# Numbering the nodes 8p+k: contiguous pieces in DRAM, strided turns on chip

## The chip, the cores and the metric

The kernel runs on one core of one Trainium2 chip. The metric is device time in microseconds (us) of one execution, the median over several runs; lower is better. Five engines work side by side, each on its own list of instructions: TensorE (PE; its loads of the stationary operand are listed apart as PEld), VectorE (DVE), ScalarE (ACT), GpSimd (POOL) and SyncE (SP). SP, ACT and POOL issue the transfers, which run on 16 DMA engines.

## The reference

Sixteen graphs of N = 1024 nodes with C = 128 features; x is [16, 1024, 128] and adj [16, 1024, 1024] with entries 0 or 1.

```
# layer 0: gated graph network, 4 steps
h = relu(layernorm(x))
for i in range(4):
    m = adj^T @ (h @ weight[i])
    h = GRU(m, h)                       # w_ih, w_hh, b_ih, b_hh of step i
x = x + h * nodemask
# layer 1: graph convolution, 4 steps
h = relu(layernorm(x))
for i in range(4):
    h = relu(adj @ (h @ W[i]) + b[i])
    h = batchnorm over all graphs and nodes, gamma[i], beta[i]
x = x + h                               # the result
```

## The kernel before

All is done by `exact_path` (L342); `general_path` stands behind a test at the end and isn't executed with these inputs. `P = C = 128` is the number of partitions, `NB = N // P = 8` blocks of nodes, `NH = 2` halves of 512 columns (`HALF`), `BH = 4` blocks in each.

A graph's features live in two forms. *By node*: a tile of 128 partitions x 1024, partition p holding 8 nodes of 128 features, block k in columns 128k to 128k+127. *By feature* (`hT`): partition c, a column for each node, 1024 columns. Before the change, block k of the form by node holds node 128k + p in partition p, so block k of `hT` is the columns 128k to 128k+127. A load of x (`load_x`, L531), a store of the middle x (`xmid_d`, L637), its reads at the end (`fetch_x`, L955) and the stores of the result (L1004) therefore move eight (four, for halves) pieces of 512 bytes for each partition.

**Recurrent part** (45 to 1237 us of the profiled execution). Two streams, `sa` and `sb`, each work on every second graph, and `half_step` lets one aggregate while the other computes its gates. In a half-step TensorE does, for one stream, eight turns of h (`features_times` with `w` None, L491: `nc.tensor.transpose` of a block of `hT` into PSUM), the aggregation (`aggregate`, L516: stationary operand from the turned h split in two f32r parts, streaming operand the rows of adj), and, for the other, the gates (L720), 24 matmuls of two instructions each. At step 0 the turns aren't needed, since h begins in the form by node. ACT and DVE compute the gates from PSUM (L730 to L738). POOL and SP keep the order in which the code is written; the other engines are ordered by the scheduler as it builds the program.

Around that, per graph: the rows of adj are first copied in DRAM (`copy_rows`, L556, by POOL) and loaded from there (`load_rows`, L562, by SP); the first two graphs load them directly (`load_rows_first`, L549). At step 1 `transpose_rows` casts each of the eight row tiles to bf16 on POOL (L575, two buffers `half1`), SP turns it with a transposing DMA (L576) into `adjT`, and POOL stores `adjT` (L775). The next graph's x is loaded by POOL (L531), normalised (`norm`, L586 to L597), and turned into the form by feature (`turn`, L611, copied from PSUM by ACT, L612). When a graph is done, `tail_norm` turns its h back (L621), multiplies by the mask and adds x (L624), stores the middle x (L637), normalises it and stores that as `ymid_d` (L641), in rows of 4 KB. VectorE also looks whether adj's values are exact (`look`, L570).

**Convolution part** (1237 to 1846 us). Four layers over all 16 graphs: SP loads the stored adjT (L873), DVE and ACT widen it (L878, L876), TensorE multiplies by the weights (L493) and aggregates (L516, L503); a barrier for the batch norm follows each layer. In the last layer `fetch_x` reads the middle x back.

**Tail** (1846 us to the end). The last h is scaled (L897), turned (L1001), added to the middle x (L1003), and SP stores it in 32 transfers of 256 KB (L1004).

The tag `x` of the pool `keep` has four buffers (`flat`): x of the first graphs, the weights `w_g` at the start, later x of the following graphs.

Of the kernel before, what the change touches and what calls it, by code (L numbers as in the profile page):

```python
# [8 lines left out]
F32 = mybir.dt.float32  # L9
# [7 lines left out]
P = 128  # L17
HALF = 512
# [323 lines left out]
def exact_path(  # L342
# [21 lines left out]
    nc = tc.nc  # L364
    B, N, C = x.shape
    L = g_weight.shape[0]
    NB = N // P
    NH = N // HALF
    BH = HALF // P
# [4 lines left out]
    dram = ctx.enter_context(tc.tile_pool(name="dram", bufs=1, space=bass.MemoryType.DRAM))  # L374
# [7 lines left out]
    def tmp(name):  # L382
        return ps_t.tile([P, HALF], F32, tag="tmp", name=name)

    adjT_d = [dram.tile([P, NB, N], BF16, tag=f"adjT{b}", name=f"adjT_d{b}") for b in range(B)]
    xmid_d = [dram.tile([N, C], F32, tag=f"xmid{b}", name=f"xmid_d{b}") for b in range(B)]
    ymid_d = [dram.tile([P, N], F32, tag=f"ymid{b}", name=f"ymid_d{b}") for b in range(B)]

    def flat(name):
        return keep.tile([P, NB, C], F32, tag="x", name=name, bufs=4)  # L390
# [4 lines left out]
    def half_tile(name):  # L395
        return keep.tile([P, N], BF16, tag="half", name=name, bufs=8)

    def turned_tile(name):
        return keep.tile([P, NB, N], BF16, tag="adjT", name=name, bufs=1)
# [5 lines left out]
    ident = const.tile([P, P], F32, tag="ident", name="ident")  # L405
# [10 lines left out]
    maskT = const.tile([P, B * NB], F32, tag="maskT", name="maskT")  # L416
# [14 lines left out]
    def load_small(prep):  # L431

        vn = prep.tile([P, C], F32, tag="vn", name="vn", bufs=1)[:NV, :]
        r0 = 0
        for src in (g_b_ih, g_b_hh):
            nc.scalar.dma_start(vn[r0 : r0 + 3 * L, :], src.rearrange("l (g c) -> (l g) c", c=C))
            r0 += 3 * L
        for src in (c_b, c_gamma, c_beta):
            nc.scalar.dma_start(vn[r0 : r0 + L, :], src)
            r0 += L  # L440
        mn = prep.tile([P, P], F32, tag="mn", name="mn", bufs=1)
        nc.scalar.dma_start(mn, nodemask.rearrange("b (k p) -> (b k) p", p=P))
        return vn, mn

    def turn_small(vn, mn):
        pt = tmp("pt_v")
        nc.tensor.transpose(pt[:, :NV], vn, ident[:NV, :NV])
        nc.vector.tensor_copy(vecs, pt[:, :NV])
        nc.vector.tensor_add(brz, vecs[:, : 3 * L], vecs[:, 3 * L : 6 * L])
        pt = tmp("pt_m")  # L450
        nc.tensor.transpose(pt[:, :P], mn, ident)
        nc.vector.tensor_copy(maskT, pt[:, : B * NB])

    wns = {}
# [29 lines left out]
    def features_times(w, hT, hw, g, name):  # L484

        pt = tmp(f"hw_{name}_{g}")
        for q in range(BH):
            j = g * BH + q
            src = hT[:, j * P : (j + 1) * P]
            if w is None:  # L490
                nc.tensor.transpose(pt[:, q * P : (q + 1) * P], src, ident)  # L491
            else:
                nc.tensor.matmul(pt[:, q * P : (q + 1) * P], src, w, start=True, stop=True)  # L493
        cols = slice(g * HALF, (g + 1) * HALF)
        nc.scalar.copy(hw[0][:, cols], pt)  # L495
        nc.vector.tensor_sub(hw[1][:, cols], pt, hw[0][:, cols].bitcast(F32))  # L496
# [28 lines left out]
    with ExitStack() as st:  # L525
# [2 lines left out]

        def load_x(b, eng):
            xt = flat(f"x{b}")  # L530
            eng.dma_start(xt, x[b].rearrange("(k p) c -> p k c", p=P))  # L531
            return xt

        raws = {}

        def gru_row(b, j):
            if j < 6:
                return row_tile(f"row{b}_{j}")
            return work.tile([P, N], F32R, tag="row2", name=f"row{b}_{j}", bufs=4)

        def load_rows_first(b, stage):

            fs = []
            for j in range(NB):
                if j < 4:
                    f = stage[:, 2 * j : 2 * j + 2, :].rearrange("p a n -> p (a n)")
                else:
                    f = work.tile([P, N], F32, tag="h", name=f"first{b}_{j}", bufs=7)
                nc.sync.dma_start(f, adj[b][j * P : (j + 1) * P, :])  # L549
                fs.append(f)  # L550
            return fs

# [5 lines left out]
        def load_rows(b):  # L558
            ts = []
            for j in range(NB):  # L560
                t = gru_row(b, j)
                nc.sync.dma_start(t.bitcast(F32), raws[b][j * P : (j + 1) * P, :])  # L562
                ts.append(t)
            return ts

# [6 lines left out]
        def transpose_rows(b, row, j, adjT):  # L572

            t = work.tile([P, N], BF16, tag="half1", name=f"half{b}_{j}", bufs=2)
            nc.gpsimd.tensor_copy(t, row.bitcast(F32))  # L575
            nc.sync.dma_start_transpose(adjT[:, :, j * P : (j + 1) * P], t)  # L576

        def norm(xt, y, name):
# [3 lines left out]
        def norm_stats(xt, name):  # L582
            stats = small.tile([P, NB, 6], F32, tag="ln_st", name=f"st_{name}")
            mv = small.tile([P, NB, 2], F32, tag="ln_mv", name=f"mv_{name}")
            for k in range(NB):
                nc.vector.bn_stats(stats[:, k, :], xt[:, k, :])  # L586
                nc.vector.bn_aggr(mv[:, k, :], stats[:, k, :])
            return mv
# [14 lines left out]
        def turn(y, name, hT=None):  # L603

            if hT is None:
                hT = work.tile([P, N], F32, tag="h", name=f"h_{name}", bufs=7)
            for hf in range(NH):
                pt = tmp(f"pt_{name}_{hf}")
                for q in range(BH):
                    k = hf * BH + q  # L610
                    nc.tensor.transpose(pt[:, q * P : (q + 1) * P], y[:, k * P : (k + 1) * P], ident)  # L611
                nc.scalar.copy(hT[:, hf * HALF : (hf + 1) * HALF], pt)  # L612
            return hT

        def tail_norm(b, xt, hT):

            for hf in range(NH):
                pt = tmp(f"pt_x{b}_{hf}")
                for q in range(BH):
                    k = hf * BH + q  # L620
                    nc.tensor.transpose(pt[:, q * P : (q + 1) * P], hT[:, k * P : (k + 1) * P], ident)  # L621
                for q in range(BH):
                    k = hf * BH + q
                    nc.vector.scalar_tensor_tensor(  # L624
                        xt[:, k, :],
                        pt[:, q * P : (q + 1) * P],
                        maskT[:, b * NB + k : b * NB + k + 1],
                        xt[:, k, :],
                        ALU.mult,
                        ALU.add,  # L630
                    )
            mv = norm_stats(xt, f"mid{b}")
            if b + 1 < B:
                y = work.tile([P, N], F32, tag="h", name=f"y_mid{b}", bufs=7)
            else:
                y = xt.rearrange("p k c -> p (k c)")
            nc.gpsimd.dma_start(xmid_d[b].rearrange("(k p) c -> p k c", p=P), xt)  # L637

            def rest():
                norm_apply(xt, y, f"mid{b}", mv)  # L640
                nc.gpsimd.dma_start(ymid_d[b], y)  # L641

            return rest
# [157 lines left out]
        with tc.tile_pool(name="prep", bufs=1) as prep, tc.manual_schedule(engines=every):  # L801


            pt = tmp("pt_idle")
# [54 lines left out]
    pt = tmp("pt_flag")  # L859
# [74 lines left out]
    xo = []  # L934

    def by_node(d, hf):
        return d.rearrange("(k p) c -> p k c", p=P)[:, hf * BH : (hf + 1) * BH, :]

    def fetch_x(b):

        if b == 2:
            ts = [flat(f"xo{k}").rearrange("p k c -> p (k c)") for k in range(4)]
            xo.extend([t[:, :HALF], t[:, HALF:]] for t in ts)
        elif b == B - 1:
            for k in range(4, 8):
                xo.append([half_tile(f"xo{k}_{hf}").bitcast(F32) for hf in range(NH)])
            ts = [keep.tile([P, N], F32, tag="row", name=f"xo{k}", bufs=12) for k in range(8, 12)]
            wide = turned_tile("xo12").rearrange("p a n -> p (a n)").bitcast(F32)
            ts += [wide[:, k * N : (k + 1) * N] for k in range(4)]
            xo.extend([t[:, :HALF], t[:, HALF:]] for t in ts)  # L950
        else:
            return
        for k in range(0 if b == 2 else 4, len(xo)):
            for hf in range(NH):
                nc.gpsimd.dma_start(xo[k][hf].rearrange("p (k c) -> p k c", c=C), by_node(xmid_d[k], hf))  # L955

    stats = small.tile([P, B * NH, 6], F32, tag="bn_st", name="stats0")
    hw, waiting = first_split(0), None
# [35 lines left out]
    for b in range(B):  # L994
        hT = conv_input(b, L, aff)
        for hf in range(NH):
            tag = turns[(b * NH + hf) % len(turns)]
            pt = tmp(f"pt_o{b}_{hf}") if tag == "tmp" else acc(tag, f"pt_o{b}_{hf}")
            for q in range(BH):
                k = hf * BH + q  # L1000
# [56 lines left out]
```

## Time and profile before

| | |
|---|---|
| median of 3 runs | 1886.74 us (1886.47 to 1887.95) |
| the profiled execution's own time | 1884.96 us |
| its span, first to last instruction | 1883.2 us |
| granted TensorE clock, mean | 0.986 |
| moved by DMA | 381.21 MB, 267824 packets, 149716 of them under 512 B |
| HBM read, written | 287.39 MB, 117.44 MB |

Medians of the transfers that the change touches, from issue to landing:

| transfer | line | queue | count | KB each | us |
|---|---|---|---|---|---|
| x, first two graphs | L531 | SP | 2 | 512 | 4.9 |
| x, the others | L531 | POOL | 14 | 512 | 5.7 |
| middle x, stored | L637 | POOL | 16 | 512 | 4.1 |
| middle x, read | L955 | POOL | 32 | 256 | 6.4 |
| result, stored | L1004 | SP | 32 | 256 | 3.7 |
| rows of adj from the copy | L562 | SP | 112 | 512 | 6.1 |

How to read the profile: the span is cut into 40 slices, each digit the busy share of an engine in tenths. In a row of a group stand line, engine, operation, output<-inputs (streaming operand first, for TensorE), shape and count; after the first bar the busy time in us and the mean ns of one; after the second the idle time of the engine ahead of them and what ended it. PE's ends are modelled, since matmuls are pipelined: the distance between starts tells what a matmul costs. In a row of a stretch stand its bounds, its length, the busy time of the five rows of engines with their counts, the granted clock, the mean share of the DMA engines and the GB/s moved.

### The profile page before, as it was taken

Reading aid. Unit: us, or ns where it says so; the run is one execution under the profiler, and the core shown is the slowest. Engines: PE = TensorE matmul, PEld = TensorE weight load, DVE = VectorE, ACT = ScalarE, POOL = GpSimd, SP = SyncE. Lnnn points to the kernel's source line nnn. Section 1 sums busy time; section 2 is a strip of 40 time slices with the busy share of each in tenths; the row PEclk is TensorE's granted clock in tenths of the full one; section 3 lists DMA queues with packets and bytes.
Section 4 is the critical chain, followed back from the end, with each engine's and each line's share of the span. In section 5 each row is a group of like instructions: output and inputs, shape, how many; then the busy total and the mean of one; then the engine's idle time right before and its main releaser. Section 6 shows DMA issues by size and latency. Waiting matters only on the chain.

```text
span 1883.2 us, 21902 instructions
## 1 busy us (share of the span) xinstructions
PE 1826.3 (97%) x7324; PEld 1259.9 (67%) x7324; DVE 1209.0 (64%) x2235; ACT 1041.8 (55%) x1561; POOL 287.5 (15%) x369
## 2 busy tenths in 40 slices
PE   7999999999999999999999999999989989989995
PEld 4666656666656566656665666667768878878884
DVE  5746864865784685595586476576656656665664
ACT  4354563563545454445456353476767767767764
POOL 3130230231141032033023012010100000000021
PEclk8999999999999999999999999999999999999997
DMA  7487476385386476557547536269956757675768
GB/s 258 120 229 255 157 203 216 140 223 170 134 256 189 147 190 202 200 168 234 190 157 203 208 114 169 85 220 319 305 187 214 246 179 246 223 247 180 250 208 259
DMA packets 267824, 381.21 MB, mean 202 GB/s; under 512 B 149716, under 2 KB 171896, under 8 KB 263864
## 3 DMA queue, kind: packets, MB, share of 16 engines
q1 hardware_dynamic: 250032, 246.21, 43.2%
q0 software_dynamic: 17456, 133.45, 20.2%
q8 instruction: 59, 0.97, 0.2%
q14 instruction: 61, 0.50, 0.1%
q10 hardware_dynamic: 216, 0.08, 0.0%
HBM read 287.39 MB, written 117.44 MB: 215 GB/s over the span
## 4 chain that ended last, share of the span: by engine, by line
PE 44%; issue 5%; DMA 3%; DVE 2%; POOL 1%; ACT 1%; SPq 0%; DVEq 0%; POOLq 0%; ACTq 0%
PE pc_m L516 12%; PE pc_g_r L516 5%; PE pc_g_z L516 5%; PE pm L516 5%; PE hw_c L493 5%; PE g_z L720 2%; PE g_r L720 2%; DMA adjT<-half 2%; PE g_xn L720 1%; PE g_hn L720 1%; PE pt_o L1001 1%; PE pw_g_hn L931 1%; PE pw_g_xn L931 1%; PE pc_g_r L503 1%; PE hw_g L491 0%
## 5 line engine op out<-in xcount | busy, mean ns | idle before, releaser
L516 PE MATMUL pm<-row,ghw 128*128 128x512 f32 x2048 | 505.0, 403 | 1.7 <-ACT ghw L697 1.7
L516 PEld LDWEIGHTS pm<-row,ghw 128*128 128x128 f32 x2048 | 383.4, 188 | 107.0 <-issue 31.6
L516 PE MATMUL pc_m<-wide,chw 128*128 128x512 f32 x1024 | 247.6, 396 | 0.0
L516 PEld LDWEIGHTS pc_m<-wide,chw 128*128 128x128 f32 x1024 | 190.7, 189 | 41.5 <-issue 3.8
L733 ACT ACTIVATE r<-r,vecs 128x512 f32<-128x512 f32 x128 | 92.3, 721 | 203.5 <-DVE r L732 203.4
L516 PE MATMUL pc_g_r<-wide,chw 128*128 128x512 f32 x464 | 185.8, 400 | 0.0
L516 PE MATMUL pc_g_z<-wide,chw 128*128 128x512 f32 x464 | 180.8, 390 | 0.0
L575 POOL CAST half<-row 128x1024 bf16<-128x1024 f32 x128 | 139.9, 1109 | 248.8 <-DMA adjT<-half 167.8
L878 DVE CAST wide<-packed 128x1024 fp32r<-128x1024 bf16 x160 | 110.5, 694 | 81.9 <-PE pc_m L516 62.4
L878 DVE CAST wide<-block 128x1024 fp32r<-128x1024 bf16 x160 | 110.4, 693 | 80.0 <-PE pc_g_z L516 42.2
L734 ACT ACTIVATE z<-g_z,brz 128x512 f32<-128x512 f32 x128 | 87.4, 683 | 121.5 <-PE g_z L720 121.5
L496 DVE TENSOR_TENSOR ghw<-hw_g,ghw 128x512 fp32r<-128x512 f32 x96 | 61.7, 683 | 122.7 <-ACT ghw L495 122.7
L720 PE MATMUL g_xn<-m,w_mT 128*128 128x512 f32 x256 | 131.7, 596 | 3.9 <-DVE r L732 3.9
L876 ACT CAST wide<-packed 128x1024 fp32r<-128x1024 bf16 x96 | 100.6, 1048 | 60.7 <-PE pc_g_z L516 30.1
L876 ACT CAST wide<-block 128x1024 fp32r<-128x1024 bf16 x96 | 100.6, 1048 | 60.2 <-PE pc_m L516 34.0
L720 PE MATMUL g_r<-m,w_mT 128*128 128x512 f32 x256 | 131.2, 594 | 0.0
L570 DVE TENSOR_REDUCE low<-row 128x1 f32<-128x1024 uint16 x112 | 130.9, 1201 | 0.0
L720 PE MATMUL g_z<-m,w_mT 128*128 128x512 f32 x256 | 130.7, 592 | 0.0
L730 ACT ACTIVATE r<-g_r,brz 128x512 f32<-128x512 f32 x128 | 87.8, 686 | 61.1 <-PE g_r L720 60.0
L736 DVE TENSOR_TENSOR h<-h,r 128x512 f32<-128x512 f32 x96 | 69.6, 725 | 78.7 <-ACT r L733 78.7
L731 DVE SCALAR_TENSOR_TENSOR r<-g_hn,vecs,r 128x512 f32<-128x512 f32 x128 | 95.1, 743 | 36.4 <-PE g_hn L720 19.1
L708 ACT COPY m<-pm 128x512 f32<-128x512 f32 x128 | 68.1, 583 | 89.4 <-PE pm L516 89.4
(128 smaller groups left out, 2767.8 us busy)
## 6 DMA issues: line engine op xcount, KB each, us to landing
packed<-adjT_d SPq DMA_DIRECT2D x256, 256.0 KB, 5.7
block<-adjT_d SPq DMA_DIRECT2D x256, 256.0 KB, 5.3
raw<-in_adj_dram POOLq DMA_DIRECT2D x112, 512.0 KB, 11.6
row<-raw SPq DMA_DIRECT2D x112, 512.0 KB, 6.1
adjT_d<-adjT POOLq DMA_DIRECT2D x16, 2048.0 KB, 7.2
xmid_d<-x POOLq DMA_DIRECT2D x16, 512.0 KB, 4.1
y<-ymid_d POOLq DMA_DIRECT2D x16, 512.0 KB, 6.1
xo<-xmid_d POOLq DMA_DIRECT2D x32, 256.0 KB, 6.4
```

Source lines behind the costliest of these rows:

```text
L493: nc.tensor.matmul(pt[:, q * P : (q + 1) * P], src, w, start=True, stop=True)
L516: nc.tensor.matmul(pm[hf], hw[s][:, j * P : (j + 1) * P], rows[j][:, hf * HALF : (hf + 1) * HALF], start=(j == 0 and s == 0), stop=(j == N ...
L570: nc.vector.tensor_reduce(low[:, k : k + 1], lows, axis=AX.X, op=ALU.max)
L575: nc.gpsimd.tensor_copy(t, row.bitcast(F32))
L720: nc.tensor.matmul(po, wT[:, i, g * C : (g + 1) * C], rhs, start=start, stop=stop)
L730: nc.scalar.activation(r, pr, AF.Sigmoid, bias=brz[:, 3 * i : 3 * i + 1])
L731: nc.vector.scalar_tensor_tensor(r, phn, b_hn(i), r, ALU.add, ALU.mult)
L733: nc.scalar.activation(r, r, AF.Tanh, bias=b_in(i))
L734: self.last_act = nc.scalar.activation(z, pz, AF.Sigmoid, bias=brz[:, 3 * i + 1 : 3 * i + 2])
L736: nc.vector.tensor_sub(ho, hin, r)
L876: nc.scalar.copy(r, t)
L878: nc.vector.tensor_copy(r, t)
```

## The change

Nodes are numbered anew: block k holds node 8p + k in partition p. The eight nodes of a partition are then neighbours in DRAM, and x, the middle x and the result move in runs of 4 KB (halves: 2 KB) for each partition; `xmid_d` takes the shape [128, 1024]. The rows of adj in row tile j become the rows 8p + j (`row_block`), 32 KB apart, 4 KB each as before.

The columns of `hT` keep the nodes' order, so a block of `hT` in the recurrent part is every eighth column (`block`). The turns of h (L491, L621) read it so; the copy after the turn of y (L612) writes every eighth column; the cast on POOL (L575) reads every eighth element of a row, so that the transposing DMA and all that follows it find block by block. In the convolution part the columns are in the order of the blocks from the start, and its turns and matmuls stay as they were.

The mask is loaded as [16, 1024] into a buffer of the tag `x` and turned by eight small transposes in place of one of 128 x 128.

```
-    xmid_d = [dram.tile([N, C], F32, ...) for b in range(B)]
+    xmid_d = [dram.tile([P, N], F32, ...) for b in range(B)]
...
+    def block(t, k):
+        return t.rearrange("c (p k) -> c k p", k=NB)[:, k, :]
+
+    def row_block(a, j):
+        return a.rearrange("(p k) n -> k p n", k=NB)[j]
...
-        mn = prep.tile([P, P], F32, tag="mn", name="mn", bufs=1)
-        nc.scalar.dma_start(mn, nodemask.rearrange("b (k p) -> (b k) p", p=P))
+        mn = flat("mask").rearrange("p k c -> p (k c)")[:B, :]
+        nc.scalar.dma_start(mn, nodemask)
...
-        nc.tensor.transpose(pt[:, :P], mn, ident)
+        for k in range(NB):
+            nc.tensor.transpose(pt[:, k * B : (k + 1) * B], block(mn, k), ident[:B, :B])
...
-                nc.tensor.transpose(pt[:, q * P : (q + 1) * P], src, ident)
+                nc.tensor.transpose(pt[:, q * P : (q + 1) * P], block(hT, j), ident)
...
-            eng.dma_start(xt, x[b].rearrange("(k p) c -> p k c", p=P))
+            eng.dma_start(xt, x[b].rearrange("(p k) c -> p k c", k=NB))
...
-                nc.sync.dma_start(f, adj[b][j * P : (j + 1) * P, :])
+                nc.sync.dma_start(f, row_block(adj[b], j))
...
-                nc.sync.dma_start(t.bitcast(F32), raws[b][j * P : (j + 1) * P, :])
+                nc.sync.dma_start(t.bitcast(F32), row_block(raws[b], j))
...
-            nc.gpsimd.tensor_copy(t, row.bitcast(F32))
+            by_block = row.bitcast(F32).rearrange("p (q k) -> p k q", k=NB)
+            nc.gpsimd.tensor_copy(t.rearrange("p (k q) -> p k q", k=NB), by_block)
             nc.sync.dma_start_transpose(adjT[:, :, j * P : (j + 1) * P], t)
...
-                nc.scalar.copy(hT[:, hf * HALF : (hf + 1) * HALF], pt)
+                by_block = hT.rearrange("c (p k) -> c k p", k=NB)[:, hf * BH : (hf + 1) * BH, :]
+                nc.scalar.copy(by_block, pt.rearrange("c (k p) -> c k p", p=P))
...
-                    nc.tensor.transpose(pt[:, q * P : (q + 1) * P], hT[:, k * P : (k + 1) * P], ident)
+                    nc.tensor.transpose(pt[:, q * P : (q + 1) * P], block(hT, k), ident)
...
-                        maskT[:, b * NB + k : b * NB + k + 1],
+                        maskT[:, k * B + b : k * B + b + 1],
...
-            nc.gpsimd.dma_start(xmid_d[b].rearrange("(k p) c -> p k c", p=P), xt)
+            nc.gpsimd.dma_start(xmid_d[b], xt.rearrange("p k c -> p (k c)"))
...
     def by_node(d, hf):
-        return d.rearrange("(k p) c -> p k c", p=P)[:, hf * BH : (hf + 1) * BH, :]
+        return d.rearrange("(p k) c -> p k c", k=NB)[:, hf * BH : (hf + 1) * BH, :]
...
-                nc.gpsimd.dma_start(xo[k][hf].rearrange("p (k c) -> p k c", c=C), by_node(xmid_d[k], hf))
+                nc.gpsimd.dma_start(xo[k][hf], xmid_d[k][:, hf * HALF : (hf + 1) * HALF])
```

More of the change, by code (lines that the diff above doesn't have):

```diff
@@ L385, in exact_path @@
     adjT_d = [dram.tile([P, NB, N], BF16, tag=f"adjT{b}", name=f"adjT_d{b}") for b in range(B)]
-    xmid_d = [dram.tile([N, C], F32, tag=f"xmid{b}", name=f"xmid_d{b}") for b in range(B)]
+    xmid_d = [dram.tile([P, N], F32, tag=f"xmid{b}", name=f"xmid_d{b}") for b in range(B)]
     ymid_d = [dram.tile([P, N], F32, tag=f"ymid{b}", name=f"ymid_d{b}") for b in range(B)]
+    def block(t, k):
+        return t.rearrange("c (p k) -> c k p", k=NB)[:, k, :]
+    def row_block(a, j):
+        return a.rearrange("(p k) n -> k p n", k=NB)[j]
     def flat(name):
@@ L488, in features_times @@
             j = g * BH + q
-            src = hT[:, j * P : (j + 1) * P]
             if w is None:
-                nc.tensor.transpose(pt[:, q * P : (q + 1) * P], src, ident)
+                nc.tensor.transpose(pt[:, q * P : (q + 1) * P], block(hT, j), ident)
             else:
-                nc.tensor.matmul(pt[:, q * P : (q + 1) * P], src, w, start=True, stop=True)
+                nc.tensor.matmul(pt[:, q * P : (q + 1) * P], hT[:, j * P : (j + 1) * P], w, start=True, stop=True)
         cols = slice(g * HALF, (g + 1) * HALF)
```

## The prediction

> **What bounds the kernel now.** I read the page's shares first, then the chain that ended last, the timeline of one half-step, the groups by shape, and last the stretches of the tail.
>
> ```profile
> span 1883.2 us, 21902 instructions
> PE 1826.3 (97%) x7324; PEld 1259.9 (67%) x7324; DVE 1209.0 (64%) x2235; ACT 1041.8 (55%) x1561; POOL 287.5 (15%) x369
> PE   7999999999999999999999999999989989989995
> DMA  7487476385386476557547536269956757675768
> ```
>
> TensorE is busy in nine tenths or more of all slices but the first, the last and three at the layer ends late in the run. Between 100 and 1225 us, the recurrent part, it is busy 1120.4 of 1125 us. An instruction that takes TensorE longer there adds its time to the run; work on another engine costs nothing until it runs out of slack. In the last slice TensorE falls to 5 while DMA stands at 8: the run ends on transfers. So the change touches two places on the path: the turns of h, and the tail.
>
> The timeline of TensorE in one half-step shows what a turn costs (start, length, then line and shape):
>
> ```profile
> 1115.93 1.03 PE L491 MATMUL hw_g<-ident,h 128*128 128x128 f32 x8
> 1116.81 1.02 PE L720 MATMUL g_r<-h_in,w_hhT 128*128 128x512 f32 x2
> ...
> 1115.70 1.02 PEld L491 LDWEIGHTS hw_g<-ident,h 128*128 128x128 f32 x8
> ```
>
> Eight turns take 0.88 us until the next matmul starts, 110 ns each. The identity streams (it is named first, as row is in pm<-row,ghw) and h is the operand that is loaded, so the step of eight falls on the weight load. There are eight loads for eight matmuls and nothing else in the group to hide a longer load behind.
>
> The groups by shape give the counts of what the change touches, all reading or writing in unbroken runs today:
>
> ```profile
> L491 PEld LDWEIGHTS hw_g<-ident,h 128*128 128x128 f32 x384 | 44.7, 140 | 7.0 <-issue 0.5 <-DVE w_mT L481 0.2
> L621 PEld LDWEIGHTS pt_x<-ident,h 128*128 128x128 f32 x128 | 15.0, 140 | 2.2
> L575 POOL CAST half<-row 128x1024 bf16<-128x1024 f32 x128 | 139.9, 1109 | 248.8 <-DMA adjT<-half 167.8 <-issue 78.0 <-ACT rs_in L592 2.4
> L612 ACT COPY h_in<-pt_in 128x512 f32<-128x512 f32 x32 | 17.3, 589 | 48.4 <-PE pt_in L611 42.2 <-DMA row<-raw 3.3 <-issue 2.9
> L570 DVE TENSOR_REDUCE low<-row 128x1 f32<-128x1024 uint16 x112 | 130.9, 1201 | 0.0
> ```
>
> The tail, in stretches (length, PE, PEld, DVE, ACT, POOL busy, clock, DMA share, GB/s), with one stretch of the first convolution layer ahead of it for comparison:
>
> ```profile
> 1262.00:1300.00 38.00, 38.00 (x154) 28.59 (x153) 25.60 (x36) 27.24 (x36) 2.89 (x6) 1.00 0.96 352
> 1852.00:1857.00 5.00, 4.88 (x40) 4.03 (x38) 5.00 (x10) 5.00 (x6) 0.00 (x0) 1.00 0.96 284
> 1862.00:1867.00 5.00, 3.63 (x28) 2.68 (x26) 5.00 (x10) 2.61 (x3) 0.00 (x0) 1.00 0.96 284
> 1867.00:1872.00 5.00, 0.00 (x0) 0.00 (x0) 1.27 (x3) 0.00 (x0) 0.00 (x0) 0.56 0.99 286
> 1872.00:1877.00 5.00, 0.00 (x0) 0.00 (x0) 0.00 (x0) 0.00 (x0) 0.00 (x0) 0.50 0.96 286
> ```
>
> The last addition ends at 1868.3 us; from there to 1880 only the result's transfers run. At the same DMA share (0.96) 512-byte pieces move 284 to 286 GB/s, and the mix of 2 and 4 KB pieces of the convolution layer moves 352.
>
> **The result (L1004), on the path: gains 6.5 us.** 32 transfers of 256 KB are 8.39 MB. At 286 GB/s they need 29.3 us, which fits: issues begin at 1849.2, the bytes flow from about 1850.6 and stop at 1880. In 2 KB pieces at 352 GB/s the same bytes need 23.8 us, 5.5 less. At 404, which is what the median 2 KB packet of the trace would give (81 ns, 16 engines), they need 20.8, 8.5 less. Below that the additions bind: 32 of them from 1848.4 to 1868.3, 0.62 us for each 256 KB, and the last transfer then needs the 2.4 us of the quickest landing. I take 366 (352 divided by its share of 0.96), 22.9 us, hence 6.4, and 0.1 for the x of the last items (L955), whose reads drain sooner. SP's issues stay ahead: those of 128 pieces (L562, L873) took 0.32 us. The low end is nothing, if writes of 2 KB should run no faster than those of 512 bytes.
>
> [...] The rows differ by 23% at equal DMA share, so the rows decide.
>
> **The first x (L531 on SP), on the path: gains 0.5 us.** VectorE's first statistics start at 5.0 us, released by x0, and the start hangs on VectorE in order (statistics, then the checks of the rows up to 26.7 us). x0 is 512 KB: 1.8 us at 286 GB/s, 1.4 at 366; its issue falls from 0.50 us to the 0.33 of the row loads (L549). That is 0.4 to 0.6 us. The 14 later loads of x go out on POOL and VectorE waited for them 16.7 us in all, but TensorE waited for none of that; nothing is counted.
>
> **The turns of h (L491, L621), on the path: the term that decides.** 384 + 128 = 512 loads now take one element of every 32 bytes. No instruction of this trace reads with such a step. The nearest row is the check of the rows (L570): it takes every second 16-bit word, in 1201 ns for 1024, 1.17 ns each, less than the unbroken VectorE additions of 512 take (L1003: 0.68 us, 1.33 ns each). By that row the low end is nothing. The high end: each load takes its 140 ns once more, all 512 on the path, 72 us. Below nothing is excluded, since no element less is loaded. I take nothing, because a load of 128 columns in a cadence of 110 ns fetches 1.2 columns a ns while the f32r matmuls of L516 stream 512 columns in 0.227 us (32 of them in 7.27 us in the chain), 2.3 a ns: the load runs at half the pace at which the array fetches operands elsewhere in this trace, and may have room for a fetch per column. It is a choice, and the range keeps the other end.
>
> [...]
>
> **Beside the path.** The cast on POOL (L575) reads by eights: 1.0 us now; by the L570 row nothing, by the high end twice, 1.1 us more. Queued behind it are SP's turning transfers (L576) and, after these, SP's row loads (L562). From the timeline of SP, the 16 turning transfers of a round run from 675.3 to 737.3 and the row loads begin at 751.8, the other rounds alike: 14 us of slack. With two buffers half of a longer cast shows per row, so sixteen rows give 8 times the addition: 8.8 us, inside the 14. Without that cover it would be the excess, in each of 7 rounds. The copy of the turned y on ACT (L612) writes by eights: 32 x 0.59 us, at most 19 us more on an engine that is 55% busy, 0.6 us at a time, queued ahead of the copies of m (L708), for which TensorE's loads waited 13.0 us in all, at most 0.5 at once; nothing. The mask: eight small turns in place of one at 19.7 us, in TensorE's gap until 26.9; uncovered, 7 x 0.33 = 2.3 us. xmid's store (L637) and the reads of x (L531, L955) become shorter POOL issues (0.92 and 0.75 us to the 0.55 of ymid's); POOL is not on the path. The row loads take rows 32 KB apart instead of neighbours, in the same 4 KB pieces: nothing, and they hide behind the matmuls except the first eight.
>
> **Sum.** The profiled execution took 1884.96 us, 1.76 beyond its span of 1883.2, and lies 1.78 under the median of 1886.74. 1884.96 - 6.5 - 0.5 = 1877.96; with 1.78 that is 1879.7.
>
> **The rivals.**
>
> The strided load is slow (ends slower). If the 110 ns cadence of a turn becomes twice that, all but the first of each group pays: 48 groups of 8 and 32 of 4 make 512 - 80 = 432, times 110 ns = 47.5 us; less 7.0, 1927.2. With 140 ns on all 512, 1951.4. It decides from 14 ns a turn (7.0 / 512), and makes the run slower by over 0.2% from 21 ns. For it: no other work hides it, TensorE is 99.6% busy there. Against it: the pace argument above. 0.36, some of it with small prices between 1890 and 1927.
>
> The strided cast on POOL is slow. From 14 / 8 = 1.75 us more, a cast of 2.8 us, SP's row loads come late and TensorE waits: at 4 us a cast 8 x 2.9 - 14 = 9 us in each of 7 rounds, 65 us, about 1945. For it: the transfers on POOL's and SP's queues keep order. Against: it needs nearly three times the present duration. 0.06.
>
> The result's writes do not speed up, or the turns cost about 10 ns: -0.5 to -3 us, 1884 to 1886. The 352 GB/s row is mostly reads, which speaks for it; ymid's stores in 4 KB pieces land in 3.0 us and xmid's in 512-byte pieces in 4.1, equal bytes, which speaks against. 0.06.
>
> **How the numbers follow.** A measurement of this kernel tells a change from none at about 0.2%, 3.8 us. Forecast 0.52, its own range 1875 to 1883; no measurable change 0.06; slower 0.42. 1875 takes in the 404 GB/s end and leaves about 0.04 below. Up to 1935 lie the first rival at up to double the cadence with some margin, about 0.28; what is beyond, near 0.14, is left out. The predicted time is that of the forecast.
>
> **What would show it.** Right: the loads of L491 and L621 stay near 140 ns, eight turns take 0.9 us, the half-step keeps its 18.4 us, and from 1850 on the tail moves over 350 GB/s and ends some 6 us sooner. Wrong: loads of 200 ns or more, the spacing of the turns growing with them, and the end of the recurrent part after 1260 us instead of 1237; or casts beyond 2.8 us with row loads issued late; or a tail still near 286 GB/s.

## The result, and the profile after

| | before | after |
|---|---|---|
| median | 1886.61 us (4 runs) | 1918.56 us (4 runs) |
| ratio to before | | 1.0165, 95% interval 1.0152 to 1.0177 |
| the profiled execution's own time, its span | 1884.96, 1883.2 us | 1917.27, 1915.5 us |

The kernel became 32 us slower. The time lies inside the stated range, but on the other side from the forecast, and neither the named first rival nor the second as described is the cause.

The page of after, its shares and the DMA engines by slices:

```profile
span 1915.5 us, 21832 instructions
PE 1838.8 (96%) x7331; PEld 1265.7 (66%) x7331; DVE 1284.9 (67%) x2235; ACT 1058.1 (55%) x1561; POOL 402.6 (21%) x369
PE   7999999999999999999999999999989989998996
DMA  7477475475376457557547535339857675765677
```

VectorE is busy 76 us more than before and POOL 115 us more, with as many instructions as before (2235 and 369). The last gate matmul of the recurrent part starts at 1275.4 us in place of 1236.9: 38.5 us are lost ahead of it.

The groups by shape that answer to those shown of before (line numbers have moved by 9 to 11):

```profile
L500 PEld LDWEIGHTS hw_g<-ident,h 128*128 128x128 f32 x384 | 49.5, 192 | 23.9 <-issue 15.7 <-PE pm L525 4.9 <-DVE w_mT L491 0.2
L632 PEld LDWEIGHTS pt_x<-ident,h 128*128 128x128 f32 x128 | 16.7, 191 | 1.4 <-DVE h L749 0.2
L585 POOL CAST half<-row 128x1024 bf16<-128x1024 f32 x128 | 273.1, 2159 | 173.8 <-DMA adjT<-half 109.7 <-issue 63.4 <-POOL half L585 0.7
L623 ACT COPY h_in<-pt_in 128x512 f32<-128x512 f32 x32 | 34.2, 1184 | 31.1 <-PE pt_in L621 24.9 <-DMA row<-raw 3.4 <-issue 2.9
```

The accesses by eights show: the weight load 191 ns for 140, the cast 2159 for 1109, ScalarE's copy 1184 for 589. But the timeline of TensorE has the eight turns as close as ever:

```profile
680.68 1.05 PE L500 MATMUL hw_g<-ident,h 128*128 128x128 f32 x8
681.57 1.02 PE L731 MATMUL g_r<-h_in,w_hhT 128*128 128x512 f32 x2
```

0.89 us from the first turn to the next matmul, where before had 0.88. What is new stands on VectorE, in the three operations that end a gate step, and not in the addition just ahead of them (L743, whose other input is in PSUM). The listing of each line gives the shortest, median and longest of its instructions in ns:

```profile
L747 DVE TENSOR_TENSOR h<-h,r x96: 669/692/3871, 86.9 to 1276.7; 128x512 f32<-128x512 f32 x96
L747 DVE TENSOR_TENSOR h<-h_in,r x32: 666/692/5031, 45.5 to 1162.6; 128x512 f32<-128x512 f32 x32
L748 DVE TENSOR_TENSOR h<-h,z x128: 650/692/4973, 46.4 to 1277.5; 128x512 f32<-128x512 f32 x128
L749 DVE TENSOR_TENSOR h<-h,r x128: 666/691/2507, 47.1 to 1278.2; 128x512 f32<-128x512 f32 x128
L743 DVE TENSOR_TENSOR r<-g_xn,r x128: 670/691/694, 44.0 to 1275.2; 128x512 f32<-128x512 f32 x128
```

Same operation, same shape, same median of 691 or 692 ns; but the three with both inputs in SBUF reach 2.5 to 5.0 us, and the one that reads PSUM never exceeds 0.694. In this trace all 55 of the three operations' instructions that take over 0.75 us overlap a cast on POOL (in before all 42); 26 of the additions of L743 overlap one too, and none of these exceeds 0.693 us. The timeline shows one such case, on POOL and VectorE (start, length):

```profile
1178.52 4.12 POOL L585 CAST half<-row 128x1024 bf16<-128x1024 f32 x2
...
1179.33 3.87 DVE L747 TENSOR_TENSOR h<-h,r 128x512 f32<-128x512 f32 x1 [0.60 <-ACT r L744]
```

Two casts run from 1178.52 to 1182.64; the subtraction that began inside them ends at 1183.20, 0.56 us after them. Here it stands until POOL is done. Behind it on VectorE wait the rest of that gate step and the next one's, and TensorE waits in turn. Its waits from 40 us to the end of the recurrent part (us in all, times, longest; two rows of before, then four of after) come to 32.4 us in place of 4.4. Two rows are new, the turns' wait for the end of the gate step and the gates' wait for the copy of m on ScalarE, which itself waited 271.6 us for VectorE's addition L743 in place of 203.4:

```profile
PE g_xn L720 <- DVE r L732: 3.9, 8, 0.6
PE g_hn L720 <- DVE r L731: 0.5, 2, 0.3
PE hw_g L500 <- DVE h L749: 15.3, 13, 2.3
PE g_r L731 <- ACT m L719: 10.7, 7, 1.6
PE g_xn L731 <- DVE r L743: 3.5, 6, 0.6
PE g_hn L731 <- DVE r L742: 2.9, 5, 0.9
```

That is 28 of the 38.5 us. The other 10 stand in no row of the waits; TensorE's busy time, whose ends are modelled, is 12.5 us longer.

The tail did what was forecast (columns as before; GB/s last):

```profile
1894.00:1899.00 5.00, 4.84 (x38) 3.89 (x38) 5.00 (x9) 5.00 (x5) 0.00 (x0) 1.00 0.99 382
1899.00:1904.00 5.00, 4.83 (x37) 3.67 (x35) 5.00 (x9) 3.88 (x4) 0.00 (x0) 1.00 0.99 381
1904.00:1909.00 5.00, 0.02 (x1) 0.00 (x0) 2.53 (x5) 0.00 (x0) 0.00 (x0) 0.69 0.97 363
```

From the first store's issue to the end it takes 28.1 us (1887.4 to 1915.5) where before took 34.0.

### The profile page after: what moved, and what is told of

It reads as the page before. It is cut to its first block, busy times and chain, and to the rows that moved or that the text cites. A ratio compares the mean times of both kernels' runs of the same rounds, so it can differ in the third digit from the quotient of the medians.

```text
span 1915.5 us, 21832 instructions
## 1 busy us (share of the span) xinstructions
PE 1838.8 (96%) x7331; PEld 1265.7 (66%) x7331; DVE 1284.9 (67%) x2235; ACT 1058.1 (55%) x1561; POOL 402.6 (21%) x369
## 4 chain that ended last, share of the span: by engine, by line
PE 40%; issue 5%; DVE 5%; DMA 2%; ACT 1%; POOL 1%; DVEq 0%; POOLq 0%; ACTq 0%
PE pc_m L525 12%; PE pc_g_r L525 6%; PE pc_g_z L525 5%; PE hw_c L502 5%; PE pm L525 3%; PE g_z L731 2%; PE g_r L731 2%; DMA adjT<-half 1%; DVE low L579 1%; POOL half L585 1%; PE pt_o L1012 1%; DVE h L747 1%; PE g_xn L731 1%; PE g_hn L731 1%; PE pw_g_hn L942 1%
## 5 line engine op out<-in xcount | busy, mean ns | idle before, releaser
L585 POOL CAST half<-row 128x1024 bf16<-128x1024 f32 x128 | 273.1, 2159 | 173.8 <-DMA adjT<-half 109.7
L744 ACT ACTIVATE r<-r,vecs 128x512 f32<-128x512 f32 x128 | 92.3, 721 | 271.6 <-DVE r L743 271.6
L731 PE MATMUL g_r<-m,w_mT 128*128 128x512 f32 x256 | 133.5, 604 | 10.7 <-ACT m L719 10.7
L748 DVE TENSOR_TENSOR h<-h,z 128x512 f32<-128x512 f32 x128 | 126.9, 991 | 14.0 <-ACT z L745 8.3
L731 PE MATMUL g_xn<-m,w_mT 128*128 128x512 f32 x256 | 131.5, 595 | 3.5 <-DVE r L743 3.5
L731 PE MATMUL g_z<-m,w_mT 128*128 128x512 f32 x256 | 130.7, 592 | 0.0
L747 DVE TENSOR_TENSOR h<-h,r 128x512 f32<-128x512 f32 x96 | 80.4, 837 | 67.9 <-ACT r L744 67.9
L966 POOL DMA_DIRECT2D xo<-xmid_d x32 | 18.5, 583 | 493.7 <-DVE wide L889 447.5
```

The source lines that it names most:

```text
L585: nc.gpsimd.tensor_copy(t.rearrange("p (k q) -> p k q", k=NB), by_block)
L731: nc.tensor.matmul(po, wT[:, i, g * C : (g + 1) * C], rhs, start=start, stop=stop)
L744: nc.scalar.activation(r, r, AF.Tanh, bias=b_in(i))
L747: nc.vector.tensor_sub(ho, hin, r)
L748: nc.vector.tensor_mul(ho, ho, z)
```

## The experiments

Three theories stood at first. Theory 1: VectorE's operations with both inputs in SBUF stand while POOL casts, and the longer cast makes them stand longer; the shared read path that the expectations name is the author's guess at the reason, which no run shows. Theory 2: ScalarE's strided copy holds up the gates. Theory 3: the casts delay SP's turning transfers and so the row loads.

**The plain cast in the changed kernel.**

```
-            by_block = row.bitcast(F32).rearrange("p (q k) -> p k q", k=NB)
-            nc.gpsimd.tensor_copy(t.rearrange("p (k q) -> p k q", k=NB), by_block)
+            nc.gpsimd.tensor_copy(t, row.bitcast(F32))
```

> The changed kernel with the cast on POOL reading in unbroken runs again; the permutation of the columns in that cast is left out, nothing else. Theory 1, the shared read path: VectorE's operations with both inputs in SBUF (the three of the gate's end) stand while POOL casts, and the strided cast makes them stand longer; then they fall back from means of 880 to 1539 ns to the 695 to 822 ns of before, the cast to about 1.1 us, the recurrent part loses its 38 us, and the time is 1886.6 less the tail's 5.9 us, near 1880. Theory 2, ScalarE's strided copy (1184 ns in place of 589) holds up the gates' queue: it is untouched here, so the time stays near 1918. Theory 3, the cast delays the turning transfers and SP's row loads: 1880 too, but then VectorE's three operations keep their lengths of after.

Measured: 1881.48 us, ratio 0.9973 (0.9963 to 0.9984). The three operations' busy time falls from 369.2 to 297.1 us. Their means are 756, 742 and 735 ns as expected, but for the first operation at step 0, which stays at 1108. The cast carries the whole loss, 37.1 us, and all else in the change together gains 5.4.

**The strided cast alone**, the same edit the other way, on the kernel before.

> The kernel before with nothing but the cast on POOL reading by eights (the order of the nodes no longer fits, so part of the meaning is lost). Theories 1 and 3: all of the loss and none of the gains, about 1886.6 + 38 = 1925; by theory 1 the three VectorE operations with both inputs in SBUF rise to means of 830 to 1540 ns, while those that read PSUM stay at 684 to 743. Theory 2: 1886.6, unchanged.

Measured: 1927.14 us, ratio 1.0207 (1.0191 to 1.0222), 40 us. The means of the three operations are 1186, 866, 822 and 732 ns (the first operation has two groups), the last two under the 830 expected. Theory 2 is gone. Theory 3 falls by SP's timeline here and in after: in after the turning transfers of a round end at 603.6 and the row loads begin at 618.1, still 14.5 us later, because it is TensorE that frees the rows (SP waited 218.7 us in all for its aggregations). Six of the seven rounds look so; in the first the slack is 0.3 us, and was 1.7 in before. In no round did TensorE wait for a row: none of its waits above names one.

```profile
536.40 67.19 SPq L586 DMA_TRANSPOSE adjT<-half  x16
618.12 26.09 SPq L571 DMA_DIRECT2D row<-raw  x16
```

**The plain copy on ScalarE.**

```
-                by_block = hT.rearrange("c (p k) -> c k p", k=NB)[:, hf * BH : (hf + 1) * BH, :]
-                nc.scalar.copy(by_block, pt.rearrange("c (k p) -> c k p", p=P))
+                nc.scalar.copy(hT[:, hf * HALF : (hf + 1) * HALF], pt)
```

> The changed kernel with ScalarE's copy after the turn of the input writing in unbroken runs again (its columns then are in the wrong order; that step is left out). Theory 2: the copy falls to 589 ns and most of the 38 us come back, near 1880. Theories 1 and 3: 1915 to 1919, a gain of 3 us at most.

Measured: 1917.46 us, ratio 1.0162 (1.0146 to 1.0177): as after. The doubled copy costs nothing that can be told.

**The tail alone**, on the kernel before.

```
     def by_node(d, hf):
-        return d.rearrange("(k p) c -> p k c", p=P)[:, hf * BH : (hf + 1) * BH, :]
+        return d.rearrange("(p k) c -> p k c", k=NB)[:, hf * BH : (hf + 1) * BH, :]
...
-                nc.tensor.transpose(pt[...], hT[:, k * P : (k + 1) * P], ident)
+                nc.tensor.transpose(pt[...], hT.rearrange("c (p k) -> c k p", k=NB)[:, k, :], ident)
```

> The kernel before with the change at its end alone: the last turns read h by every eighth column, the middle x is read back and the result stored in 2 KB pieces. No cast, no copy and no load of rows is touched. The tail of after was 5.9 us shorter (34.0 to 28.1 us from the first store's issue), so all theories expect about 1886.6 - 6 = 1880.6 and the turns at their 0.85 us per eight.

Measured: 1879.96 us, ratio 0.9965 (0.9951 to 0.9978). This is the version to keep: it computes the whole result and beats both kernels, by 6.9 us against the before of its own runs. The form by feature holds the nodes in order, so the last turns alone can choose which node goes to which partition; nothing ahead of them has to change.

**The turns alone**, L491 and L621 of the kernel before reading every eighth column.

```
-                nc.tensor.transpose(pt[...], src, ident)
+                nc.tensor.transpose(pt[...], hT.rearrange("c (p k) -> c k p", k=NB)[:, j, :], ident)
```

> The kernel before with the turns of h alone reading every eighth column (the order of the nodes no longer fits, so part of the meaning is lost). All theories now: the loads rise from 140 to 191 ns, eight turns still take 0.88 to 0.90 us, and the time stays within 2 us of 1886.8. The forecast's first rival would have 1915 or more.

Measured: 1888.00 us, ratio 1.0009 (1.0000 to 1.0018). Some 1.6 us for 512 turns, 3 ns each, at the edge of what can be told (the interval reaches from nothing to 3.4 us). The loads take 191 ns, as expected, and hide.

The next question was what of the cast does the harm: how long POOL casts, the step, or something else.

**The plain cast twice**, on the kernel before, as long on POOL as one strided cast.

```
             nc.gpsimd.tensor_copy(t, row.bitcast(F32))
+            nc.gpsimd.tensor_copy(t, row.bitcast(F32))
```

> The kernel before with each unbroken cast on POOL written twice into the same tile: POOL casts for about 2 x 1.05 us a row, as long as one strided cast, but without a step. Theory 1a, what counts is how long POOL holds the read path: VectorE's three operations with both inputs in SBUF rise to means of 830 to 1190 ns and the time goes to about 1925, as with the strided cast alone. Theory 1b, the step itself is what disturbs: they stay under 850 ns and the time within 5 us of 1886.8.

Measured: 1890.13 us, ratio 1.0021 (1.0011 to 1.0032), 3.8 us. POOL casts 299.7 us in all, more than the 274.3 of the strided cast alone, which cost ten times as much. Theory 1a, the sum of POOL's casting, is refuted as to the time. The lengths fit neither theory whole: the means are 920, 869, 826 and 698 ns, two of them above the 850 of theory 1b. The longest of the three operations is 1981 ns; the author's guess, which no run settles, is that they aren't longer because the second cast writes what the first has written and POOL pauses between the two; in the run with a pause, below, the longest is 2004 ns too.

**The cast on ScalarE**, in the changed kernel.

```
-            nc.gpsimd.tensor_copy(t.rearrange("p (k q) -> p k q", k=NB), by_block)
+            nc.scalar.copy(t.rearrange("p (k q) -> p k q", k=NB), by_block)
```

> The changed kernel whole, with the strided cast moved from POOL to ScalarE. Theory 1: POOL no longer casts, so VectorE's three operations return to 690 to 700 ns each, without long ones. The time is open: without new waits near 1880, but ScalarE gets 128 casts of 1 to 2 us (134 to 270 us), each of which waits in its queue for one of two buffers that a turning transfer of 3.3 us frees, ahead of the gates; so it may well be 1890 to 1930. A rival by which the strided read of rows hurts VectorE from any engine would leave the three operations at 880 ns and more.

Measured: 2101.76 us, ratio 1.1138 (1.1121 to 1.1155). As a version it is far worse than the 1890 to 1930 expected: ScalarE casts for 261.0 us and waits 125.9 us for buffers, with the gates behind it. As a test it is clean: with these casts gone from POOL (12 others, all before 37 us, stay) none of the three operations exceeds 695 ns, though the rows are read by eights as before.

```profile
L748 DVE TENSOR_TENSOR h<-h,z 128x512 f32<-128x512 f32 x128 | 88.1, 689 | 14.4 <-ACT z L745 8.6 <-DVE h L747 0.5
L585 ACT CAST half<-row 128x1024 bf16<-128x1024 f32 x128 | 261.0, 2069 | 126.5 <-DMA adjT<-half 125.9 <-POOL row L680 0.7
```

**The candidate in PSUM**, in the changed kernel: where the inputs lie.

```
-            nc.vector.tensor_add(r, pxn, r)
-            nc.scalar.activation(r, r, AF.Tanh, bias=b_in(i))
+            nc.vector.tensor_add(pxn, pxn, r)
+            nc.scalar.activation(pxn, pxn, AF.Tanh, bias=b_in(i))
...
-            nc.vector.tensor_sub(ho, hin, r)
+            nc.vector.tensor_sub(ho, hin, pxn)
...
-            last = nc.vector.tensor_add(ho, ho, r)
+            last = nc.vector.tensor_add(ho, ho, pxn)
```

> The changed kernel, strided cast on POOL and all, with the candidate of the gates kept in its PSUM bank, so that the first and the third of VectorE's three operations have one input in SBUF and one in PSUM; the second keeps both in SBUF. Theory 1: the first and third fall to 680 to 700 ns at most, as the addition just ahead of them has it today, and only the second still stands, longer than its 991 ns, since it takes over the wait. The time falls by something, at most to 1881; against it, the bank is held some 3 us longer and the next gate's matmuls may wait for it. If where the inputs lie doesn't matter, all three stay at means of 880 and more.

Measured: 1931.69 us, ratio 1.0243 (1.0228 to 1.0259). TensorE now waits 34.0 us for the bank (L731 for L749), so the time, expected to fall, is worse than after. The operations answer the question:

```profile
L748 DVE TENSOR_TENSOR h<-h,z 128x512 f32<-128x512 f32 x128 | 132.5, 1035 | 19.2 <-ACT z L745 16.6 <-DVE st_in L596 0.2
L749 DVE TENSOR_TENSOR h<-h,g_xn 128x512 f32<-128x512 f32 x128 | 87.3, 682 | 3.0
L747 DVE TENSOR_TENSOR h<-h,g_xn 128x512 f32<-128x512 f32 x96 | 65.9, 686 | 75.8 <-ACT g_xn L744 75.5
```

The two that got a PSUM input fell to 686 and 682 ns beside the same strided casts; the one with both inputs in SBUF still stands, at 1035 ns in place of the 991 of after.

Last, whether shorter casts let VectorE in between.

**Four pieces, and two pieces**, of the strided cast, in the changed kernel.

```
-            nc.gpsimd.tensor_copy(t.rearrange("p (k q) -> p k q", k=NB), by_block)
+            halves = t.rearrange("p (k q) -> p k q", k=NB)
+            for k in range(0, NB, 2):          # two pieces: 4 in place of 2
+                nc.gpsimd.tensor_copy(halves[:, k : k + 2, :], by_block[:, k : k + 2, :])
```

> The changed kernel whole, each strided cast cut into four of 256 columns, with no wait between the four (POOL waits for its own work ahead of each row's first). Theory 1i, a VectorE operation with both inputs in SBUF stands until the cast that is running ends: pieces of about 0.55 us, stands of at most that, so the three operations average under 760 ns and the time is the 1881.5 of the plain cast, up to 1883. Theory 1ii, it stands until POOL pauses, through casts that follow each other: the four pieces of a row count as one of 2.1 us, stands of up to 2.3 us, means of 780 to 900 ns, 1895 to 1915.

> The changed kernel whole, each strided cast cut into two of 512 columns without a wait between the two. Theory 1i: stands of at most 1.05 us, as with the two plain casts a row (which cost 3.5 us), about 1885. Theory 1ii: the same as with four pieces, 1895 to 1915.

Measured: 1903.66 us, ratio 1.0101 (1.0085 to 1.0116), and 1902.73, 1.0094 (1.0079 to 1.0110). The standing does not end with a piece: with pieces of 0.65 us one operation still takes 5.8 us. The timeline of the four pieces:

```profile
221.25 5.81 DVE L749 TENSOR_TENSOR h<-h_in,r 128x512 f32<-128x512 f32 x1
221.58 4.92 POOL L587 CAST half<-row 128x256 bf16<-128x256 f32 x8
```

(The start on VectorE is drawn 0.3 us ahead of POOL's.) Eight pieces, two rows, run on to 226.50, and the subtraction ends at 227.06, 0.56 us later, as in after. So theory 1i is refuted for such cases: VectorE stood through eight casts that followed each other without a pause. But 1ii holds for few. Of the 84 operations over 0.75 us in this trace nine take 4.0 to 5.8 us, well over its 2.3, and all nine are the first of the three, L749; the other 75 take 1.23 us at most, as by 1i. The second and the third, which reached 4973 and 2507 ns in after:

```profile
L750 DVE TENSOR_TENSOR h<-h,z x128: 646/692/1061, 46.7 to 1257.8; 128x512 f32<-128x512 f32 x128
L751 DVE TENSOR_TENSOR h<-h,r x128: 661/691/1148, 47.4 to 1258.5; 128x512 f32<-128x512 f32 x128
```

What decides whether VectorE gets in between two pieces isn't shown. The times are those of 1ii, and cutting the cast brings back 15 to 16 of the 37 us, though POOL casts for longer (349.0 and 306.2 us in place of 273.1).

**Two pieces with a pause**: the second writes one block again, which is to make POOL wait for the first.

```
+            for lo, hi in ((0, 4), (3, NB)):
+                nc.gpsimd.tensor_copy(halves[:, lo:hi, :], by_block[:, lo:hi, :])
```

> The changed kernel whole, each strided cast cut in two, the second of which writes one block again that the first has written, so that POOL waits for the first ahead of the second; the price is an eighth more casting. Theory 1ii: the pause is what lets VectorE in; the longest run is a second piece and the next row's first, about 2.3 us, and the time is as with the two plain casts a row, 1884 to 1888, clearly better than two pieces without the wait. Theory 1i: no better than those, 1885 to 1887.

Measured: 1906.63 us, ratio 1.0120 (1.0104 to 1.0135). The long cases are gone, the longest of the three operations is 2004 ns, but the time is no better than without the pause. The expectation of 1ii for the time was wrong: POOL casts 368.7 us here, and some 40 operations stand for 1.0 us or a little more.

**The tail alone, with the plain cast in four pieces.**

```
-            nc.gpsimd.tensor_copy(t, row.bitcast(F32))
+            for k in range(0, N, 256):
+                nc.gpsimd.tensor_copy(t[:, k : k + 256], row.bitcast(F32)[:, k : k + 256])
```

> The kernel before with the change at its end alone, and its unbroken cast cut into four of 256 columns. Theory 1i: the stands of today (up to 2 us, 29 us in all) shrink to a quarter; TensorE waited little for them, so 1878 to 1880, at or just below the tail alone. Theory 1ii: no difference from the tail alone, 1880, or a microsecond more by the longer casting.

Measured: 1883.63 us, ratio 0.9987 (0.9978 to 0.9996), 3.7 us above the tail alone, where no theory expected more than 1. POOL casts 210.1 us in place of 141.6, and the longest of the three operations grows to 3406 ns from 2972, though the three together take 284.7 us in place of 300.8. Cutting an unbroken cast is no gain.

The kernels side by side. "Standing" is the busy time of the three operations beyond 384 x 0.691 us; "TensorE's waits" are those of its turns of h and its gates in the recurrent part; the last column is the median against that of the same kernel with one plain cast a row (before, the tail alone, or the plain cast in the changed kernel; the medians of before that ran beside them lie between 1885.99 and 1886.84 us). All but the last column are of one traced execution:

| cast | POOL casts, us | standing, us | longest, us | TensorE's waits, us | time lost, us |
|---|---|---|---|---|---|
| plain (before) | 139.9 | 28.7 | 2.7 | 4.4 | 0 |
| plain, twice | 299.7 | 63.9 | 2.0 | 7.8 | 3.8 |
| strided, alone | 274.3 | 99.7 | 5.1 | 36.2 | 40.3 |
| plain, tail alone | 141.6 | 35.5 | 3.0 | 4.6 | 0 |
| plain, four pieces, tail alone | 210.1 | 19.4 | 3.4 | 7.8 | 3.7 |
| plain, changed kernel | 139.0 | 31.8 | 2.8 | 5.2 | 0 |
| strided, four pieces | 349.0 | 61.6 | 5.8 | 15.8 | 22.2 |
| strided, two pieces | 306.2 | 85.2 | 5.3 | 21.9 | 21.3 |
| strided, two and a pause | 368.7 | 90.7 | 2.0 | 23.2 | 25.2 |
| strided (after) | 273.1 | 103.9 | 5.0 | 32.4 | 37.1 |

The loss goes with TensorE's waits: what is added to them is 0.7 to 0.9 of the time lost in every kernel but that of four strided pieces, whose traced execution, 1897.3 us, was 6.4 us faster than its median. It goes less well with the standing, of which the plain cast twice adds 35 us for 3.8 lost and the strided four pieces 30 us for 22.2. Which of VectorE's stands reach TensorE isn't settled by these runs.

Nor do they part the step from the length of one cast, since no run has an unbroken cast of 2 us: every kernel with unbroken casts loses 3.8 us at most, every one with strided casts on POOL 21.3 or more. The length alone could do it. A cast twice as long meets twice as many operations and holds each twice as long, an estimate of four times the 28.7 us of standing in before, 115 us, where 103.9 and 99.7 were measured; two casts of the old length would make twice, 57, where 63.9 were measured.

## Why the prediction was wrong

**The step that failed** is the cast on POOL, "Beside the path", booked at nothing. Its length was bounded rightly: "by the high end twice, 1.1 us more", and it was twice. What it costs was looked for in one place only, the queues behind it: "Queued behind it are SP's turning transfers (L576) and, after these, SP's row loads (L562)". That cover held, with 14.5 us of slack still there in six rounds; in the first there was hardly any in before either (1.7 us), which "the other rounds alike" overlooks, but nothing waited there. The cost, 37.1 us, came from an engine that waits for no result of the cast: VectorE's operations stand beside it, and TensorE waits for them. That the time still fell inside the stated range is luck, since its upper part was kept for slow turns. The second rival named the right instruction with the wrong mechanism, and so a point of decision, 2.8 us a cast, that 2.1 us never reached.

The trace of before showed it, in two groups that the prediction did not set beside the addition:

```profile
L737 DVE TENSOR_TENSOR h<-h,z 128x512 f32<-128x512 f32 x128 | 105.2, 822 | 14.2 <-ACT z L734 8.9 <-DVE h L736 0.5
L738 DVE TENSOR_TENSOR h<-h,r 128x512 f32<-128x512 f32 x128 | 97.0, 757 | 2.8
L737 DVE TENSOR_TENSOR h<-h,z x128: 651/692/2522, 46.6 to 1239.4; 128x512 f32<-128x512 f32 x128
L738 DVE TENSOR_TENSOR h<-h,r x128: 664/691/2718, 47.3 to 1240.2; 128x512 f32<-128x512 f32 x128
L732 DVE TENSOR_TENSOR r<-g_xn,r x128: 669/691/693, 44.3 to 1236.8; 128x512 f32<-128x512 f32 x128
```

Means of 822 and 757 ns against medians of 692 and 691 in two groups, and hardly any spread in the third, say that something holds the first two now and then. The timeline of before says what: all 42 of the three operations' instructions over 0.75 us overlap a cast on POOL, and 26 of the additions of L732 overlap one too, none of them over 0.692 us. The runs agree: with the casts on ScalarE none of the three exceeds 695 ns, and with an input in PSUM the first and the third fall from means of 837 (1539 at step 0) and 880 ns to 686 (687) and 682. How much of a cast an operation stands through isn't the same in all of them: in the run of four pieces one took 5.81 us, through eight casts. The reason isn't shown.

**The turns**, "the term that decides", did not decide. Nothing was forecast; some 1.6 us was measured, and the cadence went from 0.88 to 0.89 us for eight. So the first rival, which got 0.36, is refuted. The reason given was right only in part: the loads did slow, from 140 to 191 ns, where they were to stay near 140, and it is against "nothing else in the group to hide a longer load behind" that a load of 191 ns in a cadence of 111 hides.

**The result's stores**: 6.5 us forecast, 5.9 us in the tail of after and 6.9 in the time of the tail alone. The rate was 381 to 382 GB/s where 366 was taken, at a DMA share of 0.99 from 1894 to 1904; the additions end at 1906.5, 9 us before the end, so the transfers still set the pace. The 404 GB/s that set the low end of the range rested on 81 ns for the median 2 KB packet; in the trace of before it is 84, which makes 390. The rival of no gain is refuted.

**The first x**: 0.5 us forecast. VectorE's statistics start at 4.26 us in place of 5.00, and the first gate matmul at 38.41 in place of 38.88: 0.5 us.

**ScalarE's copy, the mask, the x of later graphs**: nothing forecast. The copy was tried and is nothing; the others were not tried apart, and the 5.4 us gained by all but the cast leave them little room: 5.9 + 0.5 - 1.6 = 4.8.

The sum of the forecast, -7.0 us, was thus right to 1.6 us for all but one term, and that term, the cast, was a loss of 37.

## What to carry to other kernels

When an instruction gets longer, ask not only who waits for its result or stands behind it in its queue, but what else runs beside it and may be held by it; here POOL's casts held the VectorE operations with both inputs in SBUF, for up to 5.0 us where the median is 0.69. A group whose mean lies well above its median in the trace is the sign (822 against 692 ns in before), and a sister group with one input in PSUM is the control (686 against 691). And where only the order of the output is to change, look for the last step that can choose it: here strided turns at the end alone brought 6.9 us, where the whole change lost 32.

## What the runs showed of the hardware that was not expected

With a step of 32 bytes the cast on POOL took 2.05 us in place of 1.04 (medians), the cast on ScalarE 2.07 in the run on ScalarE, where unbroken casts of as many elements the other way, bf16 to f32, take 1.05, and ScalarE's copy 1184 ns in place of 589. A 128-column weight load took 191 ns in place of 140, and in the run of the turns alone some 3 ns a turn showed in the time, at the edge of what can be told. Of the 84 VectorE operations over 0.75 us in the run of four pieces, 75 took 1.23 us at most, but nine stood through six to eight casts, for up to 5.1 us. And in the result's stores 512-byte pieces at a DMA share of 0.99 moved 286 GB/s (before, 1867 to 1872 us) where 2 KB pieces moved 381 to 382 (after, 1894 to 1904).
